# Seven products of quarters for q, k and v, with partial sums seeded in PSUM, in a vision-transformer tower

## The chip, the cores and the metric

The kernel runs on one core of a Trainium2 chip. The metric is the device time of one launch in microseconds, taken as the median over runs. A core has five engines that run side by side, each through its own instructions in order: TensorE (PE, matmuls; its weight loads are listed apart as PEld), VectorE (DVE), ScalarE (ACT), GpSimd (POOL) and SyncE (SP), which issues most of the DMAs. Matmuls write PSUM, which has eight banks of 128 partitions by 512 fp32 values; all other tiles are in SBUF, and DMAs move them to and from HBM.

## What is computed

The reference, cut to the parts that matter here. 16384 tokens of 256 features come from 32 blocks of 512 tokens; all data are fp32.

```python
h = tokenizer(x, W)                       # patches, DFT and a product: (4, 4096, 256): 4 sequences
z = layernorm(h)                          # input of the attention part
n = layernorm(z, ln1)
q, k, v = n @ Wq.T + bq, n @ Wk.T + bk, n @ Wv.T + bv
mem_t = decay * mem_{t-1} + k_t * v_t     # a scan over the tokens of one sequence
z2 = z + q * mem
mlp = relu(layernorm(z2, ln2) @ W1.T + b1) @ W2.T + b2
h = h + z2 + mlp
t = layernorm(h)
# router: softmax over 8 experts, the two largest, their weights brought to a sum of 1
h = h + t + sum_e combine[:, e] * (gelu(t @ w1[e] + b1[e]) @ w2[e] + b2[e])
```

## The kernel before

**Tiles and stages.** A block is 512 tokens (BLK), held as four groups of 128 (TT = 4). "tokens" layout has tokens on partitions, "features" layout has the 256 features on partitions as two halves of 128 (KD = 2) and the 512 tokens in the free direction. Three blocks are in flight: `new` is embedded and goes through q, k, v; `mid`, one block older, goes through the MLP; `old`, two blocks older, is routed to the experts. Iteration i of the main loop (i = 0 to 30) issues, by hand and in a written order for PE, DVE, ACT and SP, one stage of each of the three, with tiles of the experts between them. The last block and the rest of the experts follow after the loop.

**Experts.** Tokens are written to a buffer in HBM, sorted by expert (`scatter`, eight indirect DMAs of POOL per block). `take` works out, in some twenty small DVE instructions, which 256-row tiles are full and appends them to a list. A tile goes through `load` (expert weights `w`, rows `xh` and `xg`, from SP), `turn` (xT, ACT), `enter` (four matmuls of 128x256, then Gelu on ACT into `ge`), `leave` (four more matmuls) and `sums` (DVE's y, then two accumulating indirect DMAs of POOL into the output). `expert_step` does `turn`, `enter`, `leave` and `sums`, where `leave` is of the tile before the entered one; `slot` does a step if enough tiles are known. In a steady block there are four slots.

**One steady iteration on PE** is: five embedding products of four matmuls each (`embed`, L370), a tile, four of the eight MLP input products (`mlp_in`, L313 through `feature_mm`), a tile, the other four, the router's logits (`logits`, L575), q, k and v of `new` (`retention`, L313, twelve matmuls of 128x512), the placing of the old block's rows (`place`, L645), a tile, half of the MLP output products (`mlp_out(0)`, L509), the transposes of the retention's result (`residual`, L468), a tile, and the other half (`mlp_out(1)`).

**What DVE does around it.** `retention(m)` runs once for each half m of the output features. ACT evacuates k with its bias into `ks` in the order of the tokens in time (L433). DVE adds v's bias and multiplies by k in one instruction (L435), runs the scan (L443), keeps the last value (`carry`, L451), and adds q's bias and multiplies by the scan's result in one instruction that also brings it back to tile order (L453). `choose` finds the two largest logits (L599 to L616). After `mlp_out(0)` DVE adds its result to h (L516), then the transposed retention to z, takes the statistics, computes 1/sqrt by hand (`factors_here`), and applies them (zz, L267). After `mlp_out(1)` it does the same for h, with POOL computing the factor (`factors`, L258 and L263), and applies it (tok, L267). Then it combines the embedding products of the next block (L376, L396), sums h (`sum_up`, L479 and L480), and normalizes (zz and z, L267, again with POOL's factor).

**Changes of layout.** From block 6 on, a layout change is made by transposing DMAs: ACT splits fp32 into two 16-bit planes (`split1`, `split2`, L293; for the experts' rows it is `row`, L550), SP issues the transposing DMA into `turned` (L301), and DVE or ACT joins the planes (`join`, L307). `turned` has a single buffer, for the tokens of the experts (tokT) and for hT in turn. hT for q, k and v is joined by DVE, hT for the MLP by ACT.

**Look-ahead.** Two halves of DVE work on the next block's input (`differences`, nine instructions of 128x512, L342 and L345) stand before and after `features1`, that is before and after the join of hT for q, k and v.

**PSUM.** Pool `p_mm` has four one-bank buffers, `p_tm` three, `p_sm` one (logits, `place` and the folding of the norms' gains into the weights).

## Time and profile before

| what | us |
|---|---|
| median of 3 runs (2125.97 to 2133.95) | 2131.74 |
| time of the profiled execution | 2129.28 |
| its span, first to last instruction | 2127.5 |
| TensorE busy | 2097.2 |
| VectorE busy | 1649.1 |
| ScalarE busy | 832.9 |
| GpSimd busy | 875.7 |
| granted TensorE clock, mean | 0.996 |

The span splits into 351.4 us up to block 6's q, k and v, 1489.9 us for 24 steady blocks of 62.08 us each, and 286.2 us for the end. Busy time is the union of an engine's instructions. In the groups, a line of the profile gives the source line, the engine, the operation, out<-in, the shapes and the count, then the busy time in us and the mean of one in ns, then the idle time of the engine just ahead of these instructions and what ended it. One fp32 matmul is two instructions in the trace. In a timeline a row gives the start, the time until the end of the merged instructions, the engine and line, and in brackets the idle time before it with what ended it. Matmuls overlap a little in such rows, so the time that a stretch takes on PE is read from one start to the next.

### The profile page before, as it was taken

Reading aid. Unit: us, or ns where it says so; the run is one execution under the profiler, and the core shown is the slowest. Engines: PE = TensorE matmul, PEld = TensorE weight load, DVE = VectorE, ACT = ScalarE, POOL = GpSimd, SP = SyncE. Lnnn points to the kernel's source line nnn. Section 1 sums busy time; section 2 is a strip of 40 time slices with the busy share of each in tenths; the row PEclk is TensorE's granted clock in tenths of the full one; section 3 lists DMA queues with packets and bytes.
Section 4 is the critical chain, followed back from the end, with each engine's and each line's share of the span. In section 5 each row is a group of like instructions: output and inputs, shape, how many; then the busy total and the mean of one; then the engine's idle time right before and its main releaser. Section 6 shows DMA issues by size and latency. Waiting matters only on the chain.

```text
span 2127.5 us, 28826 instructions
## 1 busy us (share of the span) xinstructions
PE 2097.2 (99%) x8494; PEld 1475.9 (69%) x8494; DVE 1649.1 (78%) x5152; ACT 832.9 (39%) x1329; POOL 875.7 (41%) x766
## 2 busy tenths in 40 slices
PE   8999999999999999999999999999999999998999
PEld 5666666677766667776666777666677766676776
DVE  6678877888888878888888888888788888876455
ACT  1222234443334444333444433344443334442543
POOL 1022233444444344444434444443444444345444
PEclk9999999999999999999999999999999999999999
DMA  4032256765666675575677657677765766688753
GB/s 141 21 101 78 78 132 131 163 123 136 159 131 150 154 164 123 136 160 130 150 155 165 121 137 157 133 151 155 164 121 137 159 131 151 135 196 207 111 66 45
DMA packets 425533, 284.95 MB, mean 134 GB/s; under 512 B 355232, under 2 KB 391200, under 8 KB 421280
## 3 DMA queue, kind: packets, MB, share of 16 engines
q1 hardware_dynamic: 374448, 210.21, 41.6%
q0 software_dynamic: 49632, 67.39, 18.1%
q10 hardware_dynamic: 1296, 5.52, 0.9%
q8 instruction: 67, 1.10, 0.2%
q14 instruction: 90, 0.74, 0.1%
HBM read 118.36 MB, written 88.39 MB: 97 GB/s over the span
## 4 chain that ended last, share of the span: by engine, by line
PE 96%; DVE 3%; issue 1%; DMA 0%; POOL 0%; ACT 0%; SPq 0%; DVEq 0%; POOLq 0%
PE mm L313 36%; PE tm L509 20%; PE tm L370 13%; PE mm L834 11%; PE tm L851 10%; PE tm L926 1%; PE tm L468 1%; PE mm L909 1%; PE sm L575 1%; PE mm L280 1%; PE mm L134 1%; DVE ks L443 0%; DVE st L238 0%; DVE ret L453 0%; DMA out<-y,xg 0%
## 5 line engine op out<-in xcount | busy, mean ns | idle before, releaser
L874 POOL DMA_INDIRECT out<-y,xg x262 | 427.4, 1631 | 434.5 <-DVE y L870 194.6
L313 PE MATMUL mm<-hT,w_sb 128*128 128x512 f32 x1024 | 452.5, 595 | 4.2 <-issue 4.2
L509 PE MATMUL tm<-w_sb,aT 128*128 128x256 f32 x2048 | 453.5, 379 | 2.5 <-DVE h L516 2.5
L509 PEld LDWEIGHTS tm<-w_sb,aT 128*128 128x128 f32 x2048 | 388.5, 190 | 56.6 <-DVE h L516 2.9
L668 POOL DMA_INDIRECT xbuf<-row,to x248 | 244.5, 986 | 258.0 <-DVE full L729 182.5
L313 PEld LDWEIGHTS mm<-hT,w_sb 128*128 128x128 f32 x1024 | 194.8, 191 | 222.2 <-issue 208.7
L313 PE MATMUL mm<-hT,wqkv_sb 128*128 128x512 f32 x768 | 339.7, 598 | 0.0
L370 PE MATMUL tm<-wu,xv 128*128 128x256 f32 x1280 | 282.6, 379 | 0.0
L842 ACT ACTIVATE ge<-mm,w 128x256 f32<-128x256 f32 x262 | 109.4, 470 | 403.2 <-issue 349.0
L313 PEld LDWEIGHTS mm<-hT,wqkv_sb 128*128 128x128 f32 x768 | 144.0, 191 | 175.3 <-issue 165.9
L370 PEld LDWEIGHTS tm<-wu,xv 128*128 128x128 f32 x1280 | 242.7, 190 | 33.1 <-issue 0.4
L834 PE MATMUL mm<-xT,w 128*128 128x256 f32 x1048 | 251.8, 383 | 2.7 <-DVE tile_share L863 2.6
L851 PE MATMUL tm<-w,ge 128*128 128x256 f32 x1048 | 247.9, 379 | 0.9 <-ACT ge L842 0.9
L499 ACT ACTIVATE aT<-mm,vec 128x512 f32<-128x512 f32 x256 | 172.5, 684 | 184.1 <-PE mm L313 177.2
L834 PEld LDWEIGHTS mm<-xT,w 128*128 128x128 f32 x1048 | 195.4, 191 | 40.6 <-issue 17.5
L851 PEld LDWEIGHTS tm<-w,ge 128*128 128x128 f32 x1048 | 199.3, 190 | 31.5 <-issue 3.3
L827 ACT COPY xT<-xh 128x512 uint16<-128x512 uint16 x262 | 181.7, 763 | 18.8 <-DMA xh<-xbuf 16.3
L293 ACT COPY planes<-zz 128x1024 uint16<-128x1024 uint16 x100 | 99.6, 1043 | 158.9 <-issue 126.2
L258 POOL TENSOR_SCALAR rstd<-mv 128x4 f32<-128x4 f32 x62 | 41.7, 672 | 291.4 <-DVE mv L239 289.5
L868 DVE TENSOR_TENSOR y<-tm,w 128x512 f32<-128x512 f32 x131 | 90.6, 692 | 72.7 <-PE tm L851 72.2
L618 POOL TENSOR_TENSOR ex<-euler,second 128x4 f32<-128x4 f32 x32 | 34.7, 1085 | 227.8 <-DVE second L609 227.8
L433 ACT ACTIVATE ks<-mm,vec 128x512 f32<-128x512 f32 x64 | 44.0, 687 | 206.8 <-PE mm L313 206.8
(161 smaller groups left out, 2323.3 us busy)
## 6 DMA issues: line engine op xcount, KB each, us to landing
w<-in_wex SPq DMA_DIRECT2D x113, 641.5 KB
xb<-in_x SPq DMA_DIRECT2D x32, 1040.0 KB
out<-h SPq DMA_DIRECT2D x31, 512.0 KB
bank<-in_wex ACTq DMA_DIRECT2D x8, 641.5 KB
out<-y,xg POOLq DMA_INDIRECT x262
xbuf<-row,to POOLq DMA_INDIRECT x248
xh<-xbuf SPq DMA_TRANSPOSE x131
xg<-xbuf SPq DMA_DIRECT2D x131, 4.0 KB
```

What stands on the lines that cost most here:

```text
L293: nc.scalar.copy(planes[:, :, i * D : (i + 1) * D], half)
L313: nc.tensor.matmul(ps, lhsT=w[:, k, ts(m, P)], rhs=rhs[:, k, :], start=k == 0, stop=k == KD - 1)
L370: nc.tensor.matmul(ps[:, n, :], lhsT=xv[:, i, j, :], rhs=wu[:, i, j, :], start=j == 0, stop=j == J - 1)
L499: nc.scalar.activation(self.aT[:, m, :], ps, AF.Relu, bias=vec[:, MB1 + m : MB1 + m + 1])
L509: last_product[0] = nc.tensor.matmul(ps[:, i, :], lhsT=self.aT[:, k, ts(u * 2 + i, P)], rhs=w2_sb[:, k, :], start=k == 0, stop=k == KH - 1,)
L668: write = nc.gpsimd.indirect_dma_start(out=xbuf, out_offset=bass.IndirectOffsetOnAxis(ap=self.to[:, c, t : t + 1], axis=0), in_=self.row[: ...
L827: nc.scalar.copy(halves[:, :, :, 1 - i], self.xh[:, i * KD : (i + 1) * KD, :])
L834: nc.tensor.matmul(ps[:, m, :], lhsT=self.w[:, k * D + m * P : k * D + (m + 1) * P], rhs=self.xT[:, k, :], start=k == 0, stop=k == KD - 1,)
L842: nc.scalar.activation(self.ge[:, m, :], ps[:, m, :], AF.Gelu, bias=self.w[:, 5 * D + m : 5 * D + m + 1])
L851: last_product[0] = nc.tensor.matmul(ps[:, c, :], lhsT=self.ge[:, k, ts(c, P)], rhs=w[:, (2 + k) * D : (3 + k) * D], start=k == 0, stop=k ...
L868: nc.vector.tensor_tensor(y, ps, w[:, 4 * D : 5 * D].unsqueeze(1).to_broadcast([P, 2, D]), ALU.add)
L874: add = nc.gpsimd.indirect_dma_start(out=out, out_offset=bass.IndirectOffsetOnAxis(ap=self.xg[:, c, NUMBER - D : NUMBER - D + 1], axis=0), ...
```

## The change

q, k and v are each a product of a 512x256 matrix of tokens with a 256x256 matrix of weights. Cut both into quarters of 256 tokens by 128 features and 128 by 128: eight products of quarters give the result. The change uses the scheme with seven products and sums of quarters (Winograd's form of Strassen's). The sums of weights are formed once (`mix_weights`, after block 0); the sums of tokens once per block for all three (`mix_tokens`, four DVE instructions, the mixed quarters in the `planes` buffer, one quarter of hT overwritten). In `products`, the first two of the seven go to a `mm` buffer; an ACT copy writes the first into both halves of a bank of `sums` as a seed, further products are added to it by matmuls with start=False, with another ACT copy from half to half, and ACT and DVE read the four results out at the steps where they are complete. ACT adds the biases. `qkv` runs the three in four steps each, with other work of the loop between the steps. Block 0 keeps the former way. `scan` does what is left of `retention` on DVE.

PSUM is divided anew: two buffers of `p_mm`, three of `p_tm`, and three fixed banks `sums`, which the MLP input products also use; logits and `place` go to `p_tm`. The order of the main loop changes: tiles are entered and left in halves around the steps, `take` moves from the place of `place` into `mlp_out(1)`, between the statistics and the applying of tok, and with it the fetches of the tiles that it finds. The scratch for indirect DMAs is set to 8192 bytes.

```diff
-    p_mm = ctx.enter_context(tc.tile_pool(name="p_mm", bufs=4, space=bass.MemoryType.PSUM))
+    p_mm = ctx.enter_context(tc.tile_pool(name="p_mm", bufs=2, space=bass.MemoryType.PSUM))
-    p_sm = ctx.enter_context(tc.tile_pool(name="p_sm", bufs=1, space=bass.MemoryType.PSUM))
+    p_g = ctx.enter_context(tc.tile_pool(name="p_g", bufs=1, space=bass.MemoryType.PSUM))
+    sums = [p_g.tile([P, BLK], F32, name=f"sums{i}") for i in range(3)]
...
+    wqkv_mix = const.tile([P, 3, 3, P], F32)
...
+    def mix_weights():
+        w = wqkv_sb.rearrange("p w k (m q) -> p w k m q", q=P)
+        t1, t2, t4 = [wqkv_mix[:, :, i, :] for i in range(3)]
+        nc.vector.tensor_tensor(t1, w[:, :, 0, 1], w[:, :, 0, 0], ALU.subtract)
+        nc.vector.tensor_tensor(t2, w[:, :, 1, 1], t1, ALU.subtract)
+        nc.vector.tensor_tensor(t4, w[:, :, 1, 0], t2, ALU.subtract)
+        nc.vector.tensor_tensor(w[:, :, 0, 1], w[:, :, 1, 1], w[:, :, 0, 1], ALU.subtract)
...
-    def feature_mm(w, rhs, m):
-        ps = p_mm.tile([P, BLK], F32, name="mm")
+    def feature_mm(w, rhs, m, ps=None):
+        if ps is None:
+            ps = p_mm.tile([P, BLK], F32, name="mm")
...
+        def mix_tokens(self):
+            room = one.tile([P, TT, 2 * D], U16, name="planes").rearrange("p t d -> p (t d)").bitcast(F32)
+            a, b = self.hT[:, 0, :], self.hT[:, 1, :]
+            s1, s2, s4 = self.mix = [room[:, ts(i, HALF)] for i in range(3)]
+            nc.vector.tensor_tensor(s1, a[:, HALF:], b[:, HALF:], ALU.add)
+            nc.vector.tensor_tensor(s2, s1, a[:, :HALF], ALU.subtract)
+            nc.vector.tensor_tensor(a[:, HALF:], a[:, :HALF], a[:, HALF:], ALU.subtract)
+            nc.vector.tensor_tensor(s4, b[:, :HALF], s2, ALU.subtract)
+        def products(self, which, first, to, order):
+            w11, w12, w21, w22 = [wqkv_sb[:, which, k, ts(m, P)] for k in range(2) for m in range(2)]
+            t1, t2, t4 = [wqkv_mix[:, which, i, :] for i in range(3)]
+            a, b = self.hT[:, 0, :], self.hT[:, 1, :]
+            s1, s2, s4 = self.mix
+            g = sums[which].rearrange("p (n c) -> p n c", n=2)
+            bias = [vec[:, first + m : first + m + 1] for m in range(2)]
+            def add(n, lhsT, rhs):
+                nc.tensor.matmul(g[:, n, :], lhsT=lhsT, rhs=rhs, start=False, stop=True, skip_group_check=True)
+            def biased(dst, src, m):
+                nc.scalar.activation(dst, src, AF.Identity, bias=bias[m])
+            def half(n):
+                src = g[:, n, :]
+                if order:
+                    return to[0].rearrange("p (w r) -> p w r", r=TT)[:, :, ts(n, 2)], src.rearrange("p (r w) -> p w r", r=2)
+                return to[0][:, ts(n, HALF)], src
+            ps = p_mm.tile([P, 2, HALF], F32, name="mm")
+            nc.tensor.matmul(ps[:, 0, :], lhsT=w11, rhs=a[:, :HALF], start=True, stop=True)
+            nc.tensor.matmul(ps[:, 1, :], lhsT=t1, rhs=s1, start=True, stop=True)
+            nc.scalar.copy(g, ps[:, 0:1, :].to_broadcast([P, 2, HALF]))
+            p5 = three.tile([P, HALF], F32, name="p5")
+            biased(p5, ps[:, 1, :], 1)
+            yield
+            add(0, w21, b[:, :HALF])
+            add(1, t2, s2)
+            biased(*half(0), 0)
+            nc.scalar.copy(g[:, 0, :], g[:, 1, :])
+            yield
+            add(0, w22, s4)
+            add(1, w12, a[:, HALF:])
+            if order:
+                shape = [P, P, 2, 2]
+                dst = to[1].rearrange("p (w n r) -> p w n r", n=2, r=2)
+                src = g.rearrange("p n (r w) -> p w n r", r=2)
+                also = p5.rearrange("p (r w) -> p w r", r=2).unsqueeze(2).to_broadcast(shape)
+            else:
+                dst, src = to[1].rearrange("p (n c) -> p n c", n=2), g
+                also = p5.unsqueeze(1).to_broadcast([P, 2, HALF])
+            nc.vector.tensor_tensor(dst, src, also, ALU.add)
+            yield
+            add(1, t4, b[:, HALF:])
+            biased(*half(1), 0)
+            yield
+        def qkv(self):
+            self.kv = one.tile([P, KD, BLK], F32, name="kv")
+            self.ret = one.tile([P, KD, BLK], F32, name="ret")
+            self.ks = [two.tile([P, BLK], F32, name="ks") for _ in range(KD)]
+            parts = [
+                self.products(1, BK, self.ks, True),
+                self.products(2, BV, [self.kv[:, m, :] for m in range(KD)], True),
+                self.products(0, BQ, [self.ret[:, m, :] for m in range(KD)], False),
+            ]
+            for n in range(4):
+                for part in parts:
+                    if n == 0 and part is parts[-1]:
+                        yield
+                    next(part)
+                yield
+        def scan(self, m):
+            ks, at = self.ks[m], slice(m, m + 1)
+            nc.vector.tensor_tensor(self.kv[:, m, :], self.kv[:, m, :], ks, ALU.mult)
+            nc.vector.tensor_tensor_scan(
+                ks,
+                vec[:, DEC + m : DEC + m + 1].to_broadcast([P, BLK]),
+                self.kv[:, m, :],
+                0.0 if self.i % NBLK == 0 else carry[:, at],
+                ALU.mult,
+                ALU.add,
+            )
+            nc.vector.tensor_copy(carry[:, at], ks[:, BLK - 1 : BLK])
+            ret = self.ret[:, m, :].rearrange("p (r w) -> p r w", r=TT)
+            nc.vector.tensor_tensor(ret, ret, ks.rearrange("p (w r) -> p r w", r=TT), ALU.mult)
...
-            ps = feature_mm(w1_sb, self.hT, m)
+            ps = feature_mm(w1_sb, self.hT, m, sums[m % 3])
-        def mlp_out(self, u, between=None):
+        def mlp_out_steps(self, u, meanwhile=None):
-                if i and between:
-                    between()
+                if i:
+                    yield
...
                 self.norm.stats(self.h, u * 2 + i)
             if u == U - 1:
                 self.norm.factors_here() if self.i >= NS - 1 else self.norm.factors()
+                if meanwhile:
+                    meanwhile()
                 self.tok = one.tile([P, TT, D], F32, name="tok")
                 self.norm.apply(self.tok, self.h)
                 if self.i == NS:
...
+        yield
+    def run(steps):
+        for _ in steps:
+            pass
+    def expert_step(**how):
+        run(expert_halves(**how))
+    def slot_halves(known, load=True):
+        if len(tiles) - at["enter"] > LEFT and at["enter"] + 2 <= known:
+            yield from expert_halves(load=load)
-        if len(tiles) - at["enter"] > LEFT and at["enter"] + 2 <= known:
-            expert_step(load=load)
+        run(slot_halves(known, load))
...
                     ahead = blocks[i + 1].differences(xs.pop(i + 1))
                     next(ahead)
                     new.features1()
+                    if i:
+                        new.mix_tokens()
                     next(ahead)
             if i == NS - 1:
                 slot(known)
-            if old:
-                old.logits()
-            for m in range(KD):
-                new.retention(m)
-                if old and m == 0:
+            later = iter(())
+            if i:
+                qkv = new.qkv()
+                next(qkv)
+                if old:
+                    old.logits()
                     old.choose()
-            if old:
-                take(old.i + 1, old, old.place(at_once=False))
-                old.scatter(1)
-            if i + 2 < NB:
+                next(qkv)
+                tile_steps = slot_halves(known)
+                next(tile_steps, None)
+                next(qkv)
+                if old:
+                    writes = old.place(at_once=False)
+                    old.scatter(1)
+                run(tile_steps)
+                if i + 2 < NB:
+                    xs[i + 2] = load_x(i + 2)
+                if old:
+                    old.scatter(2, last_product[0])
+                next(qkv)
+                later = slot_halves(known, load=False)
+                next(later, None)
+                next(qkv)
+                for m in range(KD):
+                    new.scan(m)
+                mid.mlp_out(0)
+                if old:
+                    old.scatter(3, last_product[0])
+            else:
                 xs[i + 2] = load_x(i + 2)
-            slot(known)
-            if old:
-                old.scatter(2, last_product[0])
-            if mid:
-                mid.mlp_out(0)
-            if old:
-                old.scatter(3, last_product[0])
+                for m in range(KD):
+                    new.retention(m)
             new.residual()
-            slot(known, load=False)
+            run(later)
             if old:
                 old.scatter(4, last_product[0])
-            if at["enter"] == 0:
-                advance("load", 2)
             if i == 0:
                 fold(w1_sb.unsqueeze(1), G2, B2, MB1)
+                mix_weights()
             else:
                 new.split2()
             if at["enter"]:
                 advance("load", at["enter"] + AHEAD - 1)
             if mid:
-                mid.mlp_out(1)
+                mid.mlp_out(1, meanwhile=lambda: old and take(old.i + 1, old, writes))
+            if at["enter"] == 0:
+                advance("load", 2)
         last, mid, old = blocks[NS], blocks[NS - 1], blocks[NS - 2]
         embed = last.embed()
...
                 expert_step()
             if m == KH - 3:
                 last.features1()
+                last.mix_tokens()
         next(weights)
         old.logits()
         old.choose()
         expert_step()
         writes = old.place()
         next(weights)
-        last.retention(0)
+        qkv = last.qkv()
+        next(qkv)
+        next(qkv)
         mid.mlp_out(0)
+        next(qkv)
         next(weights)
         take(NS - 1, old, writes)
         expert_step()
+        next(qkv)
         mid.mlp_out(1)
+        next(qkv)
         next(weights)
-        last.retention(1)
+        for m in range(KD):
+            last.scan(m)
         mid.features3()
         next(weights)
         expert_step()
...
-    nc = bacc.Bacc("TRN2", target_bir_lowering=False, num_devices=1)
+    nc = bacc.Bacc("TRN2", target_bir_lowering=False, num_devices=1, dynamic_dma_scratch_size=8192)
```

More of the change, by code (lines that the diff above doesn't have):

```diff
@@ L63, in vit_tower_kernel @@
     BLK = TT * P
+    HALF = BLK // 2
     U = TT // 2
@@ L211, in fold @@
         nc.gpsimd.tensor_copy(columns[:, :, 0], vec[:, b : b + KD])
-        ps = p_sm.tile([P, n * M, G], F32, name="sm")
+        ps = p_mm.tile([P, n * M, G], F32, name="mm")
         for i in range(n):
@@ L529, in mlp_out @@
                 nc.vector.scalar_tensor_tensor(self.by[:, 1, :], mean, -1.0, rstd, ALU.mult, ALU.mult)
+        def mlp_out(self, u, between=None, meanwhile=None):
+            for _ in self.mlp_out_steps(u, meanwhile):
+                if between:
+                    between()
         def store(self):
@@ L570, in logits @@
         def logits(self):
-            self.lg = p_sm.tile([P, TT, G], F32, name="sm")
+            self.lg = p_tm.tile([P, TT, G], F32, name="tm")
             for k in range(KD):
@@ L642, in place @@
             oh = self.oh
-            ps = p_sm.tile([P, 2, TT, E], F32, name="sm")
+            ps = p_tm.tile([P, 2, TT, E], F32, name="tm")
             for i in range(2):
@@ L958, in advance, with expert_halves @@
             at[what] += 1
-    def expert_step(fetch=True, sums=True, load=True):
+    def expert_halves(fetch=True, sums=True, load=True):
         n = at["enter"]
```

## Prediction

> **What bounds the kernel now.** I read the page first (busy shares, then the chain that ended last), then the groups by form for prices, then the timeline of one steady block, engine by engine.
>
> ```profile
> PE 2097.2 (99%) x8494; PEld 1475.9 (69%) x8494; DVE 1649.1 (78%) x5152; ACT 832.9 (39%) x1329; POOL 875.7 (41%) x766
> ...
> PE 96%; DVE 3%; issue 1%; DMA 0%; POOL 0%; ACT 0%; SPq 0%; DVEq 0%; POOLq 0%
> ```
>
> TensorE never rests, so matmul time removed is worth its full price at most. That is an average, though; the question is how far behind the next engine is. The prices:
>
> ```profile
> L313 PE MATMUL mm<-hT,wqkv_sb 128*128 128x512 f32 x768 | 339.7, 598 | 0.0
> L370 PE MATMUL tm<-wu,xv 128*128 128x256 f32 x1280 | 282.6, 379 | 0.0
> L453 DVE SCALAR_TENSOR_TENSOR ret<-mm,vec,ks 128x512 f32<-128x512 f32 x64 | 70.6, 1104 | 0.0
> L435 DVE SCALAR_TENSOR_TENSOR kv<-mm,vec,ks 128x512 f32<-128x512 f32 x64 | 47.9, 748 | 54.9 <-PE mm L313 54.9
> ```
>
> One block, from its first q/k/v matmul (1282.60) to the next (1344.68), lasts 62.08 us, and 24 such blocks fill the stretch from 351.44 to 1841.30 (1489.86 = 24 x 62.08). In it:
>
> ```profile
> 1282.60 10.57 PE L313 MATMUL mm<-hT,wqkv_sb 128*128 128x512 f32 x24
> ...
> 1296.60 7.07 PE L509 MATMUL tm<-w_sb,aT 128*128 128x256 f32 x32
> 1303.50 1.04 PE L468 MATMUL tm<-ident,ret 128*128 128x128 f32 x8
> ```
> ```profile
> 1303.71 0.69 DVE L516 TENSOR_TENSOR h<-tm,h 128x512 f32<-128x512 f32 x1 [0.34 <-PE tm L509]
> ...
> 1314.94 0.69 DVE L516 TENSOR_TENSOR h<-tm,h 128x512 f32<-128x512 f32 x1 [0.32 <-PE tm L509]
> ...
> 1319.58 1.38 DVE L267 TENSOR_SCALAR tok<-h,mv,rstd 128x256 f32<-128x256 f32 x4 [2.74 <-POOL rstd L263]
> ...
> 1330.53 1.38 DVE L267 TENSOR_SCALAR zz<-h,mv,rstd 128x256 f32<-128x256 f32 x4 [1.84 <-POOL rstd L263]
> ...
> 1334.73 1.46 DVE L307 COPY tokT<-turned 128x512 uint16<-128x512 uint16 x4
> ...
> 1341.76 1.48 DVE L307 COPY hT<-turned 128x512 uint16<-128x512 uint16 x4 [0.42 <-DMA turned<-planes]
> ```
>
> The reader should see a second loop, almost as long as TensorE's. After the first MLP output half (TensorE done at 1303.50, call it M) VectorE runs nearly unbroken until tokT is joined (1336.19). Only then can SyncE issue the next transposing DMA, because tokT and hT share the one buffer "turned" (issue at 1336.25). It lands, VectorE joins hT (1341.76, call it J), and the next q/k/v may start. M to J is 38.26 us. q/k/v needs only the first half of that join, 0.7 us, and then M is 20.90 us later (1282.60 to 1303.50): a loop of about 60, hidden under TensorE's 62.08 by 2 us. VectorE is 50.65 us busy in that window.
>
> **The change, part by part.** All sums are against the profiled execution: span 2127.5, time 2129.28, which is 2.5 below the median of 2131.74.
>
> Matmuls. 768 passes of 512 columns cost 339.7 us, 0.442 each; 1280 of 256 columns cost 282.6, 0.221 each, so halves carry no penalty. Seven products for eight in 31 of 32 blocks: 339.7 x 31/32 / 8 = 41.1 us less, 1.33 per block; TensorE alone would need 60.75 per block.
>
> ScalarE. Per block three 512-wide copies (L379: 0.585) and twelve 256-wide ones (L842: 0.470) replace two of 0.687: 7.4 - 1.4 = 6.0 us more on 25.75. The first seed is ready at 0.86 + 0.2 + 0.58 = 1.65 us after the group's start and used at 4.92, since logits, the first q products and a tile's products lie between; a tile also covers each later step. Cost nothing; without a tile between (blocks 2 to 4) about 0 to 1 us.
>
> VectorE. Four token mixes (L144, the same shape, 0.418), three sums into k, v, q (0.69 to 1.10), two products k*v (0.69), two of ret (0.69 to 1.10) replace 2 x (0.748 + 1.104) = 3.70: between 2.8 and 4.9 us more. The 1.10 is L453, whose steps through SBUF are 512 bytes long; 0.69 is the contiguous price. I take the low end, since the new outputs are contiguous and L435 shows that a stepped PSUM source costs only 0.06 (0.748 against L868's 0.692). The high end would lengthen the path below by 0.3 to 0.5 us per block: of 0.8 more in the k and v sums, 0.5 falls into a wait. The Trainium skill, SBUF — State Buffer, in its section on Door 1, says that accesses that leave a 16-byte line each time pay; by it the ret products, which read ks at 16-byte steps, and the k and v sums would stand at the high end, which no row of this trace shows for a read.
>
> Now the loop, with the new order. From J: join 1.36 (1341.76 to 1343.12), four mixes with their gaps 1.76, the second half of the differences 3.34 (1343.12 to 1346.46), the router's choice 2.99 (1289.54 to 1292.53): 9.45, then TensorE may place rows. TensorE's second product needs the first mix (J + 1.36 + 0.45 + 0.06), so its group starts, in effect, at J + 1.43; 12 quarter products at 0.4315 (20 take 8.63 at L370), logits 0.57 and one tile half of four products, 1.73 (1304.38 to 1306.11), bring it to J + 8.9. So it waits about 0.55 there. Then 0.2 + tile half 1.73 + six products 2.59 + tile half 1.73 + three products 1.29 + 16 MLP products 6.90: M = J + 23.95. VectorE meanwhile: place 2.3, a tile's output 1.7 and three sums 2.2 end at J + 16.1; ScalarE's last halves of k and v come at J + 17.6 (third products, then three pieces of 0.42); then twice 0.72 + 1.32 + 0.07 + 0.73 for product, scan, carry and ret: J + 23.3, just in time.
>
> From M to J the instructions stand as before except: the wait of 0.32 goes, because a tile half now stands before M and TensorE is early, not VectorE; the table of the tiles (3.51, from 1298.16 to 1301.67) moves into the wait of 2.74 for POOL's rstd. That is 38.26 - 0.32 + 0.77 = 38.7. This block waited 0.42 for the landing; the mean over 25 blocks is 22.8 / 25 = 0.91: 39.2.
>
> Loop: 23.95 + 39.2 = 63.1 against 62.08, so a steady block becomes 1.0 us longer and TensorE idles 2.3 in it. 24 x 1.0 = 24 us.
>
> PSUM. Two mm buffers for four, and logits and place taking tm slots: the tile half after the transposes reuses the slot of the first MLP half, read at M + 0.96, TensorE there at M + 0.88; the second MLP half waits for the first z sum, at M + 2.75. Together 0.15, covered by the loop.
>
> Moved transfers. One tile fetch instead of two stands ahead of the turned rows on SyncE (1319.56 to 1327.74 now); rows turn earlier, which nothing waits for. The first fetch of new tiles comes a third of a block later, still some 20 us before its use. The scatters on POOL keep their number. Less scratch for indirect DMAs: POOL waited 36.7 us for landings in all and idles over half the span; I take 0, between 0 and 20 us.
>
> The ends. Blocks 1 to 5 have few or no tiles to cover the steps: their loop is as tight, and I take +4 in all (between -5 and +8: -1.3 each where covered, +1.6 where not). In the tail, token transposes follow the second MLP half after three products (1.3 us) instead of after six whole ones (5.2), and already waited 1.16: +3, between 0 and 6.
>
> Sum: 24 + 4 + 3 = 31 more: 2129.3 + 31 = 2160.
>
> **Rivals.** (1) TensorE stays the bound: the loop comes in under 60.9, for instance if the landing and the choice are each a microsecond earlier. Then 41 - 0.15 x 24 - 7 = 30 less, about 2100. It decides where the loop falls below 60.9; from the rows that takes 2.2 us. For it: 99% busy, and 78% leaves VectorE room on average. Against: the hT join waited for its DMA in all 25 blocks. Partway, loops of 61.0 to 61.6, is 2105 to 2121.
> (2) About the same: the landing always takes its shortest (1.0 to 0.5 saved per block) and the ends cost little: 2125 to 2140.
> (3) Slower still: stepped reads cost 1.10, and TensorE's idling drops its clock: 2175 to 2200. In the tail of this profile an idle 1.16 us with eight transposes behind it was followed by 3.42 us at half clock:
>
> ```profile
> 1938.83:1942.25 3.42, 3.42 (x10) 2.69 (x9) 2.33 (x5) 1.74 (x4) 0.00 (x0) 0.50 0.97 250
> ```
>
> The granted clock is the third number from the end. Once in every block that is 1.7 x 24 = 41 us; but an idle 1.50 at 251.51 left it at 1.00, so I add nothing. The Trainium skill, TensorE: Matmul & The Clock Gate, on why this matters for kernels, warns only of idle gaps over about 3 us, which would exclude it; the row differs.
>
> **How the numbers follow.** The forecast, 2143 to 2175: 0.53. Slower still: 0.08. Same: 0.16. TensorE bound or partway there: 0.23. A measurement of this kernel can tell about 0.5%, 11 us, from no change. The range goes from 2104, inside the first rival, to 2184: some 0.1 is left out on each side.
>
> **What would show it.** Right: period of steady blocks 62.5 to 63.5; TensorE idle about 1.5 us before the first mixed operand (line 509) and 0.5 before the row placing, in every block; VectorE over 54 us busy per block; tok no longer waiting for rstd; hT's join still ended by the DMA. Wrong: periods near 61 with no idle at those two places, or ScalarE named as what the seeded products wait for.

## The result, and the profile after

The changed kernel takes 2156.36 us (median of four runs, 2154.3 to 2159.63) against 2129.97 beside it: a ratio of 1.0125, 95% interval 1.0099 to 1.0151. It is slower by 26 us, and by 25 in a repeat below, where the prediction said 31, but these are made up quite differently: little of the 24 us put on the steady blocks came, and the start and the tail cost far more than the 7 put on them. That the total came out near the forecast is luck.

The page of the profiled execution (time 2159.63, span 2157.9), busy times and the chain that ended last:

```profile
PE 2089.9 (97%) x9052; PEld 1579.6 (73%) x9052; DVE 1740.5 (81%) x5373; ACT 981.2 (45%) x1732; POOL 899.5 (42%) x766
...
PE 82%; DVE 8%; DMA 6%; issue 1%; ACT 1%; POOL 1%; another core or an unknown queue 0%; SPq 0%; POOLq 0%; DVEq 0%; ACTq 0%
PE tm L615 20%; PE sums L326 13%; PE tm L383 12%; PE mm L947 10%; PE tm L964 10%; PE sums L496 8%; DMA turned<-planes 6%; PE mm L509 2%; DVE hT L319 1%; PE mm L508 1%; PE tm L1039 1%; PE tm L574 1%; PE mm L1022 1%; PE tm L688 1%; PE mm L136
```

Before, 96% of the chain was TensorE. Now 8% runs over VectorE (3% before) and 6% over one transfer, the transposed planes: that is the second loop of the prediction, come to the surface. The prices of the new operations, groups by form (busy time, mean ns | idle just before):

```profile
L496 PE MATMUL sums<-hT,wqkv_sb 128*128 128x256 f32 x372 | 110.6, 379 | 0.0
L509 PE MATMUL mm<-planes,wqkv_mix 128*128 128x256 f32 x186 | 57.8, 392 | 12.1 <-DVE planes L480 12.1
L566 DVE TENSOR_TENSOR ret<-ret,ks 128x512 f32<-128x512 f32 x62 | 67.0, 1080 | 0.0
L529 DVE TENSOR_TENSOR ks<-sums,p 128x512 f32<-128x512 f32 x31 | 21.2, 685 | 4.2 <-ACT sums L517 4.2
```

Line 509 is the first mixed operand, and the 12.1 us that it waited for the mix, 0.5 in a steady block, are most of the idle time that these blocks show. One steady block, from its first q/k/v product at 1290.85 to the next at 1352.96 (62.11 us), TensorE and then VectorE:

```profile
1290.85 0.70 PE L508 MATMUL mm<-hT,wqkv_sb 128*128 128x256 f32 x2
1292.06 0.70 PE L509 MATMUL mm<-planes,wqkv_mix 128*128 128x256 f32 x2 [0.51 <-DVE planes L480]
...
1299.41 0.20 PE L758 MATMUL tm<-both_bfloat,rc 128*128 128x32 bf16 x2
...
1313.79 1.04 PE L574 MATMUL tm<-ident,ret 128*128 128x128 f32 x8
```
```profile
1290.01 1.47 DVE L319 COPY hT<-turned 128x512 uint16<-128x512 uint16 x4 [1.45 <-DMA turned<-planes]
...
1313.99 0.69 DVE L622 TENSOR_TENSOR h<-tm,h 128x512 f32<-128x512 f32 x1 [0.28 <-PE tm L615]
...
1329.89 1.37 DVE L279 TENSOR_SCALAR tok<-h,mv,rstd 128x256 f32<-128x256 f32 x4
...
1344.87 1.46 DVE L319 COPY tokT<-turned 128x512 uint16<-128x512 uint16 x4
...
1352.11 1.46 DVE L319 COPY hT<-turned 128x512 uint16<-128x512 uint16 x4 [1.55 <-DMA turned<-planes]
```

Both joins of hT end a wait for the transfer; tok has no wait any more. From the join (J, 1290.01) to the end of the first MLP half (M, 1313.79) is 23.78 us, from there to the next join 38.32. Now the stretch of 22 steady blocks (7 to 28) as a whole, the table of windows of the kernel before and of the changed one (length, busy time of PE, PEld, DVE, ACT, POOL, then the granted clock):

```profile
413.52:1779.22 1365.70, 1365.70 (x5504) 961.95 (x5500) 1111.51 (x3524) 568.08 (x903) 602.75 (x507) 1.00 0.67 146
```
```profile
420.25:1788.18 1367.93, 1354.80 (x5897) 1032.31 (x5897) 1172.34 (x3675) 670.41 (x1189) 618.16 (x506) 1.00 0.68 145
```

22 blocks last 1367.93 instead of 1365.70: 0.1 us more each, where 1.0 was forecast. An eighth of the matmul work of q, k and v is gone and the block has not moved. So the loss lies at the ends. By place, from the starts of the first q/k/v product of a block, with the tiles done there (a tile is 16 passes of 0.216, 3.46 us):

| stretch | before | changed | changed, again | forecast |
|---|---|---|---|---|
| start to block 6 | 351.44 (6 tiles) | 357.83 (4) | 357.72 (4) | +4 |
| blocks 6 to 28, each | 62.08 | 62.19 | 62.11 | +1.0 |
| blocks 29 and 30 | 128.65 | 130.64 | 130.53 | +1.0 |
| from block 31 | 219.60 (24) | 239.03 (26) | 231.57 (26) | +3 |
| span | 2127.5 | 2157.9 | 2148.4 | +31 |

Two tiles have moved from the first stretch to the last. The table, now taken behind a block's tile slots, accounts for one of them: with the table back at its place, in a run below, the first stretch has 5. What moved the other was not isolated. With both put back (6.9 us), the first stretch is 13 us longer than before, the last 12.5 or 5. The last differs by 7.5 us between two executions of the same program. Behind its first 42 us the first stretch has two falls of the granted clock (third from the end), and the kernel before has none there:

```profile
219.30:226.10 6.80, 5.32 (x7) 2.23 (x8) 4.86 (x11) 4.49 (x7) 3.94 (x3) 0.50 0.16 33
277.30:284.10 6.80, 5.06 (x10) 3.54 (x11) 4.93 (x11) 6.19 (x9) 3.94 (x3) 0.50 0.12 26
```

What stands around the first of them, on TensorE, ScalarE and SyncE, and then the same tile in the kernel before:

```profile
211.52 5.35 PE L383 MATMUL tm<-wu,xv 128*128 128x256 f32 x24
220.78 11.49 PE L326 MATMUL sums<-hT,w_sb 128*128 128x512 f32 x20 [3.91 <-ACT hT L293]
```
```profile
218.90 1.38 ACT L940 COPY xT<-xh 128x512 uint16<-128x512 uint16 x2 [7.46 <-DMA xh<-xbuf]
220.15 1.06 ACT L293 COPY hT<-mm 128x512 f32<-128x512 f32 x2
```
```profile
215.52 1.28 SPq L917 DMA_TRANSPOSE xh<-xbuf  x1
```
```profile
208.29 1.29 SPq L804 DMA_TRANSPOSE xh<-xbuf  x1
...
211.50 1.39 ACT L827 COPY xT<-xh 128x512 uint16<-128x512 uint16 x2 [0.47 <-DMA xh<-xbuf]
```

The two kernels had started this block's q, k and v at 180.40 and 180.28. ScalarE stood 7.46 us at the turn of the first tile, whose rows had only been asked for at 215.52 (the table was ready at 213); before, they were asked for at 208.29 and the turn waited 0.47. Queued behind the turn were the hT copies that TensorE needed next. At 279.04 the same happens to the second tile: ScalarE stands 8.56 us, TensorE 5.01.

### The profile page after: what moved, and what is told of

Its sections match the earlier page's. It is cut to its first block, busy times and chain, and to the rows that moved or that the text cites. A ratio compares the mean times of both kernels' runs of the same rounds, so it can differ in the third digit from the quotient of the medians.

```text
span 2157.9 us, 30492 instructions
## 1 busy us (share of the span) xinstructions
PE 2089.9 (97%) x9052; PEld 1579.6 (73%) x9052; DVE 1740.5 (81%) x5373; ACT 981.2 (45%) x1732; POOL 899.5 (42%) x766
## 3 DMA queue, kind: packets, MB, share of 16 engines
q0 software_dynamic: 49632, 67.39, 17.6%
q8 instruction: 71, 1.16, 0.2%
## 4 chain that ended last, share of the span: by engine, by line
PE 82%; DVE 8%; DMA 6%; issue 1%; ACT 1%; POOL 1%; another core or an unknown queue 0%; SPq 0%; POOLq 0%; DVEq 0%; ACTq 0%
PE tm L615 20%; PE sums L326 13%; PE tm L383 12%; PE mm L947 10%; PE tm L964 10%; PE sums L496 8%; DMA turned<-planes 6%; PE mm L509 2%; DVE hT L319 1%; PE mm L508 1%; PE tm L1039 1%; PE tm L574 1%; PE mm L1022 1%; PE tm L688 1%; PE mm L136 1%
## 5 line engine op out<-in xcount | busy, mean ns | idle before, releaser
L987 POOL DMA_INDIRECT out<-y,xg x262 | 448.5, 1712 | 546.6 <-DVE y L983 278.6
L326 PE MATMUL sums<-hT,w_sb 128*128 128x512 f32 x1024 | 456.0, 598 | 9.1 <-ACT hT L293 9.1
L326 PEld LDWEIGHTS sums<-hT,w_sb 128*128 128x128 f32 x1024 | 196.1, 192 | 229.6 <-issue 207.8
L964 PE MATMUL tm<-w,ge 128*128 128x256 f32 x1048 | 254.0, 385 | 5.0 <-DVE y L981 5.0
L947 PEld LDWEIGHTS mm<-xT,w 128*128 128x128 f32 x1048 | 201.9, 193 | 50.0 <-issue 18.1
L605 ACT ACTIVATE aT<-sums,vec 128x512 f32<-128x512 f32 x256 | 172.4, 684 | 133.5 <-PE sums L326 125.8
L496 PE MATMUL sums<-hT,wqkv_sb 128*128 128x256 f32 x372 | 110.6, 379 | 0.0
L250 DVE BATCH_NORM_STATS2 st<-h 128x6 f32<-128x256 f32 x256 | 104.9, 410 | 3.3
L358 DVE TENSOR_TENSOR xv<-xb 128x512 f32<-128x512 f32 x160 | 104.2, 684 | 3.1 <-DMA xb<-in_x 3.1
L319 ACT COPY hT<-turned 128x512 uint16<-128x512 uint16 x100 | 66.1, 760 | 84.1 <-DMA turned<-planes 84.1
```

The source lines that it names most:

```text
L250: nc.vector.bn_stats(self.st[:, t, :], src[:, t, :])
L326: nc.tensor.matmul(ps, lhsT=w[:, k, ts(m, P)], rhs=rhs[:, k, :], start=k == 0, stop=k == KD - 1)
L496: nc.tensor.matmul(g[:, n, :], lhsT=lhsT, rhs=rhs, start=False, stop=True, skip_group_check=True)
L605: nc.scalar.activation(self.aT[:, m, :], ps, AF.Relu, bias=vec[:, MB1 + m : MB1 + m + 1])
L947: nc.tensor.matmul(ps[:, m, :], lhsT=self.w[:, k * D + m * P : k * D + (m + 1) * P], rhs=self.xT[:, k, :], start=k == 0, stop=k == KD - 1,)
L964: last_product[0] = nc.tensor.matmul(ps[:, c, :], lhsT=self.ge[:, k, ts(c, P)], rhs=w[:, (2 + k) * D : (3 + k) * D], start=k == 0, stop=k ...
```

## The experiments

The theory (A): in steady blocks the loop join, mix, choice, products, first MLP half, VectorE, tokT's join, transfer, join is the bound, and the single buffer "turned" is the link that closes it; the rest of the loss is the late table (ScalarE's queue) and the order of the tail. The rival (B): TensorE's own new order is the bound, by ScalarE's seeding copies and the fewer PSUM buffers.

### The changed kernel once more

> The changed kernel once more, unaltered, so that the others of this call have its time beside them on the same chip: ratio to the kernel before 1.010 to 1.015, as before.

Measured: 2151.07 us against 2126.04 for the kernel before, ratio 1.0117 (1.0102 to 1.0133). Its stretches are the column "changed, again" above: all agree to 0.1 us (the steady blocks each) but the last.

### Two buffers for the transposed planes

```
-            self.turned = one.tile([P, TT, 2, KD, P], U16, name="turned")
+            self.turned = two.tile([P, TT, 2, KD, P], U16, name="turned")
-            self.xh = six.tile([P, 2 * KD, S], U16, name="xh")
+            self.xh = four.tile([P, 2 * KD, S], U16, name="xh")
```

> The changed kernel with two buffers for the transposed planes (turned) instead of one, and four instead of six for a tile's rows xh to make room. Theory A, the loop of VectorE and one transposing DMA bounds the steady block: the planes of hT are split 2.28 us before the DMA may be issued (1344.12 against 1346.40), so the join comes up to 2.3 us earlier, TensorE becomes the bound with 60.75 us a block, and a steady block falls from 62.19 to between 60.8 and 61.3: 21 to 33 us in 24 blocks, about 2130. Theory B, TensorE's own order bounds the steady block (copies that seed the sums, fewer PSUM buffers): the block stays at 62.2 and the time within 5 us of 2156.

Measured: 2128.43 us, ratio to the kernel before 1.001 (1.0 to 1.0021), some 23 us less than the changed kernel by the two ratios. VectorE and the DMA issues on SyncE in a steady block, and its windows (22 blocks):

```profile
1328.34 1.46 DVE L319 COPY tokT<-turned 128x512 uint16<-128x512 uint16 x4
...
1333.96 1.46 DVE L319 COPY hT<-turned 128x512 uint16<-128x512 uint16 x4
```
```profile
1327.62 1.78 SPq L313 DMA_TRANSPOSE turned<-planes  x1
```
```profile
420.19:1763.78 1343.59, 1343.59 (x5898) 1035.98 (x5896) 1169.43 (x3675) 669.17 (x1188) 615.75 (x506) 1.00 0.69 148
```

The planes go out at 1327.62, before tokT is joined, and the join of hT waits for nothing. A block is 61.07 us and TensorE has no idle in it. All of ScalarE's and VectorE's extra work is still there (669 and 1169 us busy, as in the changed kernel): theory A holds, B does not. The seeds cost the steady block nothing that shows; at most they have a part in the 0.3 us that a block still lies above the 60.75 of TensorE's work.

### The same two buffers in the kernel before

The edit is the one above, on the kernel with eight products.

> The kernel before (eight products of quarters) with two turned buffers and four xh. If the transposing loop lies 2 us under TensorE's own 62.08 there, as the prediction read it, the second buffer gives nothing: steady blocks of 62.08, within 3 us of 2126. If the two buffers help by themselves and not together with the seven products: 20 us or more less.

Measured: 2127.75 us, ratio 0.9994 (0.9983 to 1.0006); blocks of 62.08. The window of 22 blocks, TensorE busy throughout:

```profile
412.77:1778.48 1365.71, 1365.71 (x5504) 961.96 (x5500) 1107.98 (x3521) 568.87 (x903) 602.32 (x507) 1.00 0.66 145
```

The buffer is worth nothing where TensorE is the bound, the seven products nothing where the loop is the bound, and both together 1.0 us a block.

### The choice ahead of the differences

```
-                next(qkv)
                 if old:
                     old.logits()
+                next(qkv)
+                if old:
                     old.choose()
+                    next(ahead)
```

(and the same next(ahead) taken out behind the mixes, except where there is no old block).

> The changed kernel with the router's logits ahead of the first q/k/v products on TensorE, and the router's choice ahead of the second half of the differences on VectorE. Theory A: TensorE's idle 0.5 to 0.8 us before its first mixed operand is filled by the logits (0.57), the choice is done 3.3 us earlier so that placing never waits, and the first MLP half ends 0.5 us earlier after the join: 62.19 becomes about 61.7 a block, 12 us in all, about 2144. Theory B: no step of the steady block lies on that path: within 4 us of 2156.

Measured: 2155.79 us, ratio 1.0132 (1.0118 to 1.0147): nothing gained; steady blocks 62.25 on average. TensorE at the group's start:

```profile
1294.05 0.70 PE L509 MATMUL mm<-planes,wqkv_mix 128*128 128x256 f32 x2 [0.32 <-DVE planes L480]
...
1295.86 0.70 PE L508 MATMUL mm<-hT,wqkv_sb 128*128 128x256 f32 x2 [0.24 <-ACT p L499]
```

Two things ate the 0.5 us. The third product now finds its PSUM slot still held by ScalarE's copy of p, where the logits had covered that (0.24), and row placing comes 9.17 us after the join instead of 9.40: 0.23 a block, not 0.5. And in four blocks the join waited 3.0 to 3.6 us for the transfer, against 1.3 to 1.9 in the changed kernel. Why these landings are late was not found. The time is the one that B had forecast, and by itself this run would speak for B; the rows show that it is the shorter step and the late landings that cancel. The 0.5 us was an estimate of mine, twice too large.

### The table of tiles back at its place

```
                     old.scatter(1)
+                    take(old.i + 1, old, writes)
...
-                mid.mlp_out(1, meanwhile=lambda: old and take(old.i + 1, old, writes))
+                mid.mlp_out(1)
```

(with the first two fetches in front of the split again).

> The changed kernel with the table of tiles right after the row placing in every block, and the first fetches there, as in the kernel before: the move of the table alone undone. Theory A (the steady block is bound by the path join, choice, placing, sums, first MLP half, VectorE, landing): 3.3 us of table stand before the three sums that gate TensorE's fourth products, as measured in two early blocks (waits of 3.6 and 3.9 there), and tok waits 2.7 us for rstd again where the table (3.27) stood: 2.8 us more a block, 65.0 instead of 62.2, 50 to 68 us more, about 2215. The other theory, a tile half of 1.7 and six products of 2.6 us on TensorE hide the table: less than 20 us more.

Measured: 2217.63 us, ratio 1.043 (1.0414 to 1.0446); steady blocks 65.0. TensorE's fourth products and the sums on VectorE that they wait for:

```profile
1288.82 2.93 PE L496 MATMUL sums<-hT,wqkv_mix 128*128 128x256 f32 x6 [2.08 <-DVE ks L529]
```
```profile
1282.95 0.15 DVE L836 TENSOR_TENSOR full<-cnt,first 1x8 f32<-1x8 f32 x1
...
1288.08 0.69 DVE L529 TENSOR_TENSOR ks<-sums,p 128x512 f32<-128x512 f32 x1
```

In most blocks J to M grows by 2.7 us. On average it grows by 2.95, because in a few blocks, this one among them, the wait is followed by 3.4 us at half clock. M to tokT is as long as in the changed kernel (0.1 less), M to the next join 0.15 shorter: 2.8 a block in all. Moving the table into the wait for rstd is what the seven products need in the steady block, and it is also what makes the first tiles late.

### The table early for the first tiles only

The same move for blocks with i < 5.

> The changed kernel with the table of tiles taken right after the row placing again in the blocks before the sixth (i < 5), as in the kernel before, and the first two fetches there. If the late first fetch is what held ScalarE's queue at the start of blocks 4 and 5: TensorE's idle 3.91 and 5.01 us there and the 6.8 us at half clock behind each (3.4 us lost each) go, 15.7 us, less up to 5 us for a table of 2 to 3 us in two blocks with nothing to hide it: 2140 to 2148. If the two PSUM buffers left for transposed features, or the token mixes, hold those blocks: no change, 2153 to 2160.

Measured: 2145.37 us, ratio 1.0089 (1.0074 to 1.0104). The idle at the starts of blocks 4 and 5 is gone, but TensorE waits for the sums of k in two blocks (0.4 us in the changed kernel), each time with 3.4 us at half clock behind it:

```profile
193.76 2.05 PE L496 MATMUL sums<-hT,wqkv_mix 128*128 128x256 f32 x6 [3.59 <-DVE ks L529]
...
250.07 2.93 PE L496 MATMUL sums<-hT,wqkv_mix 128*128 128x256 f32 x6 [3.93 <-DVE ks L529]
```

Block 6 starts 4.2 us earlier. Without the late fetch the early stalls do not arise; this cure gives 4.2 of the 13 us back, 6 to 8 by the ratios.

### ScalarE's first turns late

```
-            if at["enter"] == 0:
-                advance("turn", 2)
...
+            if at["enter"] == 0:
+                advance("turn", 1)
...
-        advance("turn", n + 2)
+        advance("turn", n + 2 if n else 1)
         advance("enter", n + 1)
         yield
+        advance("turn", n + 2)
```

(the first turn goes behind the first MLP's activations of its block).

> The changed kernel with ScalarE's turn of the first two tiles moved behind its other work: the first tile's after the first MLP's activations of its block, the second's after the first tile's Gelu. The fetches stay late. If the only harm of the late fetch is that ScalarE stands at the turn with the hT copies queued behind it: TensorE's 3.91 and 5.01 us of idle in blocks 4 and 5 shrink to under 1.5 together, the two stretches of 6.8 us at half clock go (3.4 us lost in each), 12 to 16 us less than the changed kernel. If the hT copies themselves, through two PSUM buffers, are the cause: no change, within 4 us.

Measured: 2137.59 us, ratio 1.0058 (1.0045 to 1.0072), 13.5 us less than the changed kernel beside it. ScalarE and TensorE at the place where 3.91 us had been idle:

```profile
212.31 1.08 ACT L293 COPY hT<-mm 128x512 f32<-128x512 f32 x2
215.98 1.99 ACT L663 COPY row<-tok 128x1024 uint16<-128x1024 uint16 x2 [2.59 <-DVE tok L279]
```
```profile
212.50 5.35 PE L383 MATMUL tm<-wu,xv 128*128 128x256 f32 x24
217.69 6.60 PE L326 MATMUL sums<-hT,w_sb 128*128 128x512 f32 x15
```

The fetches are as late as in the changed kernel; only the copies no longer stand behind the turn. Behind the first 43 us no stretch at half clock is left before block 6, which starts at 346.55 instead of 357.7, with the same four tiles done. So the late fetch did harm only through the turn's place in ScalarE's queue; either edit removes the stalls.

### The tail's order

The last block's q, k and v as before: whole products around the second MLP half.

> The changed kernel with the last block's q, k and v from eight quarters again and at the places of the kernel before (whole products ahead of the first MLP half and after the second); one weight quarter is restored by one subtraction, and the last block's tokens are not mixed. If the order of the tail costs what the traces differ by there (8.0 us more waits and 10.3 us more at half clock, 5.1 lost), less 1.3 us of matmul that comes back: 11 to 13 us less, about 2144. If the two tiles that the loop no longer does (6.9 us) and the fewer PSUM buffers make the longer tail: no more than 3 us less, 2153 to 2158.

Measured: 2146.85 us, ratio 1.0097 (1.0082 to 1.0111). The last stretch is 227.08 us: 12 less than in the first execution of the changed kernel, but only 4.5 less than in the second. My 11 to 13 was the difference of two single traces of a part that varies by itself. Less the two tiles, 220.2: the kernel before to within 1 us.

### Together

The two buffers, the old tail and the late turns at once:

> Three edits of this study at once: two turned buffers, the last block's q, k and v as in the kernel before, the first two turns on ScalarE late. If they act at different places (24 steady blocks, the tail, blocks 4 and 5) they add up: two buffers alone gave 2128.4; the tail takes off 6 to 12 more by median and trace of the kernel with the old tail, less what the two buffers' own tail already lacks (229.8 against 239.0 us), so 2 to 6; the late turn 12 to 16: 2106 to 2114, faster than the kernel before by 0.6 to 0.9%. If they share one cause (the tail's waits move with the phase in which the loop hands over): 2118 to 2126.

Measured: 2115.2 us, ratio 0.9948 (0.9935 to 0.9962): faster than both kernels. Blocks of 61.07, block 6 at 345.66, but a last stretch of 230.8.

The two buffers and the late turns, the tail as the change has it:

> The changed kernel with two turned buffers and the late turn on ScalarE, the tail left as the change has it. Traces of the tail differ by up to 8 us between executions of the same kernel (239.0 and 231.6 in two of the changed one), so the old tail may have given little: 2111 to 2118. If the old tail is worth the 4.5 us by which its trace was shorter than the second of those: 2117 to 2122.

Measured: 2119.49 us, ratio 0.9955 (0.9938 to 0.9973), last stretch 234.85. The two intervals overlap almost wholly: what the old order of the tail adds to the other two edits cannot be told apart here.

One tile moved into the idle time before the token transposes, on top of the last kernel:

```
         take(NS - 1, old, writes)
-        expert_step()
         next(qkv)
         mid.mlp_out(1)
         next(qkv)
+        expert_step()
```

> The same with one tile of the tail moved from ahead of the second MLP half (block 30's) to behind it, between the last three products and the token transposes, where TensorE idles 3.7 to 3.9 us for tok with 3.4 us or more at half clock behind it. If that idle sets the tail: 3.5 of idle and 1.7 of half clock, 3 to 6 us less than without. If what follows waits for VectorE's scans and choice anyway (the next wait is for the choice of block 30's experts): within 2 us.

Measured: 2121.78 us, ratio 0.9969 (0.9957 to 0.9981): no gain. TensorE's waits in its tail, and those of the kernel without the move:

```profile
1911.25 1.64 PE L292 MATMUL mm<-ident,tok 128*128 128x128 f32 x8 [0.47 <-DVE tok L279]
...
1925.08 0.24 PE L758 MATMUL tm<-both_bfloat,rc 128*128 128x32 bf16 x2 [4.01 <-DVE both_bfloat L729]
```
```profile
1914.16 2.21 PE L292 MATMUL mm<-ident,tok 128*128 128x128 f32 x8 [4.30 <-DVE tok L279]
...
1926.04 0.21 PE L758 MATMUL tm<-both_bfloat,rc 128*128 128x32 bf16 x2 [0.25 <-DVE oh L726]
```

The 4.3 us of idle only moved to the next place at which TensorE needs VectorE.

## Why the prediction was right, and where it was not

**The sum.** 31 was 24 in the steady blocks and 7 at the ends. Measured in the two traces, blocks 6 to 30 cost 5 and 3 us more, the first stretch 6 in both, the last 19 and 12. The mechanism of the steady block was right; its size was not, and errors of opposite sign at the ends brought the total close. That is luck.

**Matmuls.** Of the 1.33 us a block less, 1.0 shows with the loop out of the way (62.08 to 61.07), 22 us over 22 blocks; the last 0.3 I have not traced.

**ScalarE.** 6.0 more a block at cost 0: busy time in the 22 blocks rose by 102 us, 4.7 a block, and the two-buffer kernel shows that it is hidden.

**VectorE.** By the rows: mixes 1.70, sums 2.05, products of k and v 1.38 and of ret 2.16, less 3.70, is 3.6 more, between my ends of 2.8 and 4.9. As busy time, where overlapping rows count once, the 22 blocks show 61 us more, 2.8 a block. The sums took the low price (0.68), the ret products the high one (1.08). The high one hurt nothing: the scans end at 1313.7, just before TensorE's M, as the sum had it.

**The loop.** The mechanism is the one forecast, and the step that failed is the size of M to J. J to M was 23.95 forecast (its terms add up to 23.9), 23.78 measured (row placing at J + 9.40 against 9.45). M to J was forecast at 39.2 and was 38.4 on average (62.18 a lap over 22 blocks of the profiled execution, less 23.78). Of the 0.8, about 0.3 is the landing: I took a mean wait of 0.91, which put tokT to the join at 6.06, and it was 5.75. About 0.5 is VectorE's stretch before it: 0.24 is the table (3.27 against 3.51), 0.17 the embedding (5.04 against 5.21), the rest is small gaps. Because the loop (63.1 forecast) stood against 62.08, an error of 0.9 in 63 removed nearly all of the 24 us. The prediction stated the margin itself: its second rival took the shortest landing and gave "about the same", and in the steady blocks that is what came out, though only 0.3 of the 0.8 is the landing. Of the signs, the period (62.5 to 63.5) and VectorE's busy time (over 54 against 53.3) were missed, tok without a wait and the join ended by the DMA were right, the idle before the first mixed operand was 0.5 instead of about 1.5, and that before row placing did not appear, because there TensorE and VectorE arrive within 0.1 us of each other.

**PSUM.** 0.15 covered: nothing shows in the changed kernel; 0.24 showed once the logits no longer covered it.

**Moved transfers.** This step was wrong in kind. "The first fetch of new tiles comes a third of a block later, still some 20 us before its use" counted to the matmul that uses the tile. Its first use is ScalarE's turn, which the program puts ahead of the hT copies at the start of the next block, and there the rows were 7.5 us late. By the rows above the fetch came some 7 us later than in the kernel before, not a third of a block, and even that was too late. The two stalls and the half clock behind them cost 11 us by the trace and 13.5 by the medians, which the late turn takes back. The smaller scratch for indirect DMAs was not tried alone.

**Early blocks** (+4 between -5 and +8): 6 by the clock, 13 with the two tiles counted. Nearly all of it is the stall above; without it the stretch is 2 us longer than before. **The tail** (+3 between 0 and 6): 12 and 19 in two executions, 5 and 12.5 without the two tiles. The forecast's reason (token transposes with three products in front of them instead of six whole ones) is there as an idle of 3.7 us, but it is not what sets the length: filling it, in the last run, gave nothing. What makes the tail longer stays open.

**Rival (1)**, TensorE bound at about 2100, was one buffer away. The two-buffer kernel is that case in every steady block, and with the late turn it gives 2119.5 rather than 2100: a block keeps 0.3 us (7 in all), and the tail costs more than the 3 that I had put there.

**Half clock.** The prediction gave nothing for it. The row of this trace is an idle of 3.91 and of 5.01 us, each with 6.8 us at 0.50; the steady idle of 0.5 us in every block left 1.00. In the kernel with the table back TensorE idles 1.9 to 2.1 us ahead of line 496 in each of 24 blocks, and behind four of these waits stand 3.41 us at 0.50. The Trainium skill, TensorE: Matmul & The Clock Gate, on why this matters for kernels, asks for no idle gaps over about 3 us; the rows of 3.91 and 5.01 agree with it. The 1.16 us of the kernel before, with eight transposes behind, and the four waits of about 2.1 us remain outside it: in these traces a gap under 3 us can still cost half clock.

**Stepped reads.** The rows: line 566 reads ks in steps of 16 bytes and takes 1.08; line 529 reads p by turns from two rows 512 bytes apart and takes 0.68, as a contiguous sum does. The Trainium skill, SBUF — State Buffer, in its section on Door 1, says that each access that crosses to a new 16-byte line pays; this agrees with line 566 and not with line 529, where the measurement decides.

## What to carry to other kernels

When the bound engine is relieved, look for the loop that closes through a single buffer and price it to the tenth of a microsecond: here 62.1 against 62.08 decided between no gain and 1.0 us a block, and a second buffer that was worth nothing before became worth 23 us. When a step moves, count to the first instruction in any in-order queue that needs its result, and see what stands behind that one; here ScalarE's copy, not the matmul, was the first user. Do not take the difference of two single traces for the price of a stretch whose own length varies.

## What the runs showed of the hardware that I had not expected

A read that alternates between two rows 512 bytes apart cost nothing (0.68 us), while a read in 16-byte steps of the same size cost 1.08. The same program's last stretch took 239.0 and 231.6 us in two executions, with 23.7 and 17.6 us at half clock in it: in the longer one ScalarE stood 5.14 us for a tile's rows and TensorE 5.17 us for the hT copies, which the other does not show. The kernel before has 4.17 us of idle at the same place. I have not settled what puts the transfers in another order there.
